# Attention beginnings in a written order, statistics, mixes and sums in other places, last batch on VectorE

## The chip, the cores and the metric

One core of a Trainium2 chip runs the whole program. Its engines are TensorE (PE in the profile; PEld is its weight load), VectorE (DVE), ScalarE (ACT), GpSimd (POOL) and SyncE (SP), which issues the DMAs. Each engine works through its own instructions in a fixed order and waits on semaphores for the others. The metric is the device time of one execution in microseconds (us): 1452.35 us, the median of three runs from 1451.99 to 1453.28. By the spread of these runs, a difference below some 0.2% can't be told from none.

## The reference

Everything is float32. x is 8 batches of 512 tokens with 512 channels (B, S, D); the context is 8 x 120 x 512. Four layers follow each other, each added to x through the tanh of a gate:

```python
x = x + jnp.tanh(g_xattn[0]) * _L0_xattn_ref(_layernorm(x), ctx, ctx, ...)       # 16 heads of 32, 120 keys
x = x + jnp.tanh(g_ffn[0])   * _L0_ffn_ref(_layernorm(x), Wc, bc, W1, b1, ...)   # routed: 32 tokens a group, 128 experts
x = x + jnp.tanh(g_xattn[1]) * _L1_xattn_ref(_layernorm(x), ctx, ctx, mask, ...) # with a mask and biases
x = x + jnp.tanh(g_ffn[1])   * _L1_ffn_ref(_layernorm(x), W_r, W_k, W_v, ...)    # mixes with the previous token:
    # xr = mu_r*x + (1-mu_r)*x_prev; out = sigmoid(xr @ W_r.T) * (square(relu(xk @ W_k.T)) @ W_v.T)
```

## The kernel before

x stays in SBUF as 32 tiles (NT) of 128 tokens by 512 channels; four tiles (TB) are a batch. Layernorm of a tile is `stats` (L372: `bn_stats` and `bn_aggr` on DVE, L49 and L50; after the fourth tile of a batch four small POOL instructions, the scales, L58 to L64) and `normalize` (L385: one ACT instruction, and in the second attention layer a POOL addition of the output bias to x, L394).

**Attention** (class CrossAttention, used twice). The constructor is its beginning. `load` issues the DMAs. `project_keys` transposes the context batch by batch (PE, L317, tile ctps), copies the result to ctxT (DVE L324 for even batches, ACT L322 for odd ones), and after each four batches makes half of the keys (PE L330, tile kps, 16 matrix products; ACT writes kT, L339 or L343). `project_values` makes the values of one batch (PE L349, tile vps; DVE L358 or L360). `prologue` interleaves values, the transposes of the first eight tiles of x (PE L405, tile xnps), the first queries and the scores of tile 0. `sum_query_weights` is four POOL instructions (L88). The key, value, transpose, query and output tiles share four PSUM banks (pool at_mm): a product waits until the bank four tiles back was read.

`run` is a loop of slots t, one for each tile of x: scores of tile t+1, queries ahead, output of tile t-1 (PE L582, DVE L591), transposes of the probabilities of tile t, its attention (PE L565, ACT aT L573). `tail` does the slots from 27 to 32, where no queries are left. Scores (L459 on): DVE takes two maxima (L498, L509), ACT exponentials (L501, L512), POOL normalizes (L491). `then` hands each slot to the next layer's `in_slot`, at stages 0 to 3 of the slot.

**Products of seven** (class SevenProducts). A 512x512x512 product is made from seven half-size ones, p1 to p7, with sums of quarters ahead (L88, L107) and additions after each (L169 to L202); two of the additions after p7 are on POOL (L191, L192). Queries, and all three products of the last layer, are made so.

**Channel mix** (class ChannelMix), the last layer. Its first batch is prepared in the last slots of the second attention (`in_slot`): key weight sums on POOL, mixes (`mix_chunk`: ACT L1161, DVE L1164), sums of the mix (L107 on DVE), p1 to p3 of the keys, sums of the other weights (`sum_weights`). It also takes the statistics of each tile two slots back. `run` then loops over the batches: keys, gates, values, where `stage` deals out the steps of a list over the seven products. `values` ends with the gate (DVE L1238), the addition to x (POOL L1241, for half of the last batch DVE) and the DMA of the result.

**Order of the work.** Inside `manual_schedule(engines=...)` the named engines get their instructions in the order of the calls. For engines that aren't named, a planner with its own costs orders them when the program is built. Before the change PE is in written order everywhere, SP in the second attention, the experts and the channel mix, and DVE, ACT and POOL only in the tails and in the channel mix's `run`; in both beginnings the planner places them.

## Time and profile before

| what | us |
|---|---|
| median of the runs | 1452.35 |
| the profiled execution, its own time | 1454.12 |
| its span | 1452.3 |
| PE busy | 1391.5 (96%) |
| DVE busy | 1021.2 (70%) |
| ACT busy | 768.9 (53%) |
| POOL busy | 653.0 (45%) |

The span is cut by stage like this: the first beginning from 0 to about 90 us, the slots of the first attention to about 475, the experts to 697, the second beginning to about 785, its slots to 1082, its tail to 1148, the channel mix to the end. In a timeline row the first number is the start, the second the length, then engine, line, operation, output and input tile, shapes and the number of instructions put together; the brackets give the engine's idle time just before and what ended it. In a row of a stretch each engine has its busy time and its instructions; the number after POOL is the granted clock of TensorE as a share of full speed, the last two are DMA.

### The profile page before, as it was taken

What the parts mean: (1) busy time and instruction counts of PE and PEld (TensorE: products, weight loads), DVE (VectorE), ACT (ScalarE), POOL (GpSimd) and SP (SyncE); (2) the same over time, 40 slices, a digit from 0 to 9 for tenths busy, and PEclk for the clock granted to TensorE, in tenths of its full rate; (3) what the DMA queues carried; (4) which work ended last, traced back from release to release, by engine and by line L of the source; (5) the groups of instructions that cost most, each with busy time, mean ns of one, the idle gap of its engine ahead of it and who ended that gap; (6) DMA issues with size and microseconds to landing.
All of it is one profiled execution on the core that took longest, in us unless ns stands there. A gap on an engine that the chain in (4) does not pass through costs nothing.

```text
span 1452.3 us, 32575 instructions
## 1 busy us (share of the span) xinstructions
PE 1391.5 (96%) x13728; PEld 1071.6 (74%) x13728; DVE 1021.2 (70%) x1449; ACT 768.9 (53%) x1874; POOL 653.0 (45%) x584
## 2 busy tenths in 40 slices
PE   6999999999999988999799999999998999999997
PEld 3477777777776777888457777777775688888886
DVE  2557767777776776777615788777779677777786
ACT  1256666666666445444225666566565554545543
POOL 2235545545544001555515676666546333333332
PEclk9999999999999999999999999999999999999999
DMA  9200000000001356433301000000000000000001
GB/s 301 100 9 23 23 23 23 24 23 23 23 23 46 125 155 206 118 103 85 115 0 59 2 1 2 1 2 2 2 30 2 1 29 29 30 30 30 30 17 43
DMA packets 44886, 69.46 MB, mean 48 GB/s; under 512 B 2891, under 2 KB 20811, under 8 KB 44739
## 3 DMA queue, kind: packets, MB, share of 16 engines
q1 hardware_dynamic: 44451, 67.37, 14.4%
q8 instruction: 108, 1.77, 0.5%
q14 instruction: 39, 0.32, 0.1%
q10 hardware_dynamic: 288, 0.00, 0.0%
HBM read 50.59 MB, written 16.78 MB: 46 GB/s over the span
## 4 chain that ended last, share of the span: by engine, by line
PE 29%; DVE 11%; ACT 5%; issue 3%; POOL 2%; POOLq 0%; DVEq 0%; ACTq 0%
PE qps L148 7%; PE ops L582 6%; PE cps L148 3%; PE tps L530 3%; PE kps L330 2%; PE vps L349 2%; PE aps L565 2%; PE s L473 2%; DVE xk L1164 2%; DVE xr L1164 1%; ACT kT L1214 1%; DVE cv L1238 1%; ACT pr L501 1%; PE xnps L405 1%; DVE xks L107 1%
## 5 line engine op out<-in xcount | busy, mean ns | idle before, releaser
L491 POOL TENSOR_TENSOR pr<-pr,rs 128x960 f32<-128x960 f32 x128 | 229.7, 1797 | 233.3 <-DVE rs L490 214.8
L582 PE MATMUL ops<-wo,aT 128*128 128x512 f32 x512 | 239.8, 595 | 3.0 <-ACT aT L573 3.0
L501 ACT ACTIVATE pr<-s,nmx 128x120 f32<-128x120 f32 x512 | 176.3, 370 | 118.2 <-DVE nmx L498 118.2
L582 PEld LDWEIGHTS ops<-wo,aT 128*128 128x128 f32 x512 | 92.0, 190 | 74.8 <-issue 67.0
L991 POOL TENSOR_TENSOR r<-r,b 128x1024 f32<-128x1024 f32 x31 | 73.6, 2378 | 145.5 <-ACT r L990 145.5
L148 PE MATMUL qps<-xnT,wq 128*128 128x256 f32 x512 | 119.6, 381 | 0.0
L530 PEld LDWEIGHTS tps<-ident,pr 128*120 128x120 f32 x864 | 96.8, 138 | 28.4 <-issue 24.8
L501 ACT ACTIVATION_READ_ACCUMULATOR pr<-s,nmx 128x1 f32 x512 | 111.1, 217 | 0.0
L509 DVE TENSOR_REDUCE mx<-s 128x8 f32<-128x960 f32 x64 | 74.0, 1156 | 51.6 <-PE s L473 51.6
L148 PEld LDWEIGHTS qps<-xnT,wq 128*128 128x128 f32 x512 | 95.7, 189 | 15.2 <-issue 1.0
L530 PE MATMUL tps<-ident,pr 128*120 128x128 f32 x864 | 104.8, 273 | 1.7 <-ACT pr L501 1.5
L49 DVE BATCH_NORM_STATS2 bnst<-x 128x6 f32<-128x512 f32 x128 | 84.5, 684 | 15.7 <-DMA x<-in_x_dram 14.3
L517 DVE TENSOR_REDUCE sm<-pr 128x8 f32<-128x960 f32 x64 | 73.6, 1149 | 23.5 <-ACT pr L512 23.5
L406 ACT COPY xnT<-xnps 128x512 f32<-128x512 f32 x64 | 38.0, 594 | 84.9 <-PE xnps L405 84.9
L565 PE MATMUL aps<-prT,v 120*32 120x128 f32 x2048 | 73.2, 278 | 4.9 <-ACT prT L555 3.0
L498 DVE TENSOR_REDUCE nmx<-s 128x8 f32<-128x960 f32 x64 | 73.4, 1147 | 5.7 <-PE s L473 5.7
L1241 POOL TENSOR_TENSOR x<-x,cv 128x512 f32<-128x512 f32 x30 | 44.0, 1466 | 72.0 <-DVE cv L1238 72.0
L511 DVE TENSOR_TENSOR pr<-s,mx 128x960 f32<-128x960 f32 x64 | 73.5, 1149 | 0.8
L540 ACT COPY prT<-tps 120x1024 f32<-120x1024 f32 x54 | 55.0, 1018 | 33.5 <-PE tps L530 33.5
L473 PE MATMUL s<-kT,qT 32*128 32x120 f32 x2048 | 71.6, 277 | 0.0
L473 PEld LDWEIGHTS s<-kT,qT 32*128 32x128 f32 x2048 | 66.3, 188 | 6.5 <-issue 6.3
L565 PEld LDWEIGHTS aps<-prT,v 120*32 120x32 f32 x2048 | 53.8, 110 | 19.1 <-issue 8.4
(184 smaller groups left out, 3111.9 us busy)
## 6 DMA issues: line engine op xcount, KB each, us to landing
w<-in_w_dram SPq DMA_DIRECT2D x32, 512.0 KB, 4.9
x<-in_x_dram SPq DMA_DIRECT2D x8, 1024.0 KB, 14.8
aside<-x SPq DMA_DIRECT2D x32, 256.0 KB, 2.0
x<-aside SPq DMA_DIRECT2D x8, 1024.0 KB, 10.2
out_dram<-x SPq DMA_DIRECT2D x14, 512.0 KB, 2.8
ctx<-in_ctx_dram SPq DMA_DIRECT2D x4, 960.0 KB, 11.7
wk<-in_wk_dram SPq DMA_DIRECT2D x3, 1024.0 KB, 11.3
wv<-in_wv_dram SPq DMA_DIRECT2D x3, 1024.0 KB, 5.9
```

The lines of the kernel that those rows point to most:

```text
L49: cm.nc.vector.bn_stats(st, cm.x[:, t, :])
L148: self.nc.tensor.matmul(ps[:, m, :], self.a[a][:, k, m * P : (m + 1) * P], self.b[b][:, k, :], start=(k == 0), stop=(k == 1),)
L473: nc.tensor.matmul(s[j // 2][:, j % 2, hc * LK : (hc + 1) * LK], self.qT[b][r : r + 32, hc, toks], self.kT[r : r + 32, hc, keys], start=no ...
L491: nc.gpsimd.tensor_tensor(pr[:, js, :, :], pr[:, js, :, :], rs[:, js, :, :].to_broadcast([P, 2, NC, LK]), ALU.mult,)
L501: nc.scalar.activation(pr[:, 2 + j, hc, :], sv[1][:, j, hc, :], AF.Exp, bias=nmx[:, j, hc, :], accum_out=sm[:, 2 + j, hc : hc + 1],)
L509: nc.vector.tensor_reduce(mx, sv[0], AX.X, ALU.max)
L511: nc.vector.tensor_tensor(pv, sv[0], mx.to_broadcast([P, 2, NC, LK]), ALU.subtract)
L517: nc.vector.tensor_reduce(sm[:, :2, :], pv, AX.X, ALU.add)
L530: nc.tensor.transpose(ps[:, jj, hc * P : (hc + 1) * P], pr[:, 2 * u + jj, hc, :], self.cm.ident,)
L565: nc.tensor.matmul(aps[32 * j : 32 * j + 32, hc, :], self.v[b // 2][:LK, b % 2, h * HD : (h + 1) * HD], prT[:, j, hc, :], start=True, stop ...
L582: nc.tensor.matmul(ops, self.aT[t][:, c, :], self.wo[:, c, :], start=(c == 0), stop=(c == NC - 1),)
L991: nc.gpsimd.tensor_tensor(r, r, b2, ALU.add)
```

## The change

No instruction is added or taken away in kind and count; they are put in other places and on other engines.

- Both beginnings are built with all five engines in written order. Statistics go by batch: batch 0 behind the last context copy in `project_keys`, batches 1 and 2 after the first normalizations, batches 3 to 7 each behind a value copy. `run` has no statistics any more. In the second beginning, scaling of the biases, of the output bias and the mask's row each get a place of their own, and the mask's DMA goes ahead of those of the output bias and of wq. The normalization of the scores of tile 0 goes behind the last two values, and the query sums of batch 1 go from POOL to DVE.
- In the last slots of the second attention, the statistics of tiles 24 to 31 go into the first four `values` of the channel mix, two tiles each. The four key mixes are spread over slots 27 (two), 28 and 29. The sums of the key mix go from DVE to POOL. The mixes and normalizations behind the keys' p5 in slot 31 go behind the attention of that slot. The sums of the value weights go from slot 32 to the start of slot 31.
- In `values` of the last batch, the two additions of p7 and all additions to x are on DVE.

```diff
@@ SevenProducts
-    def __init__(self, nc, psum, a, b, c, spare, finish=None, order="1265743", bias=None):
+    def __init__(self, nc, psum, a, b, c, spare, finish=None, order="1265743", bias=None, engine=None):
+        self.engine = engine or nc.gpsimd
...
-        nc.gpsimd.tensor_tensor(self.c[1, 1], u3, self.q5, ALU.add)
-        nc.gpsimd.tensor_tensor(u2, u2, self.q5, ALU.add)
+        self.engine.tensor_tensor(self.c[1, 1], u3, self.q5, ALU.add)
+        self.engine.tensor_tensor(u2, u2, self.q5, ALU.add)
@@ CrossAttention.__init__
                 self.load(ins, list(loads), mask, biases)
+                if self.biased:
+                    self.scale_biases()
                 self.project_keys()
-                for t in range(TB):
-                    self.stats(t)
+                if self.biased:
+                    nc.gpsimd.tensor_scalar(self.gbo, self.gbo, self.gate, None, ALU.mult)
                 for t in range(2):
                     self.normalize(t)
+                if self.masked:
+                    self.make_mask()
                 self.sum_query_weights()
+                for b in (1, 2):
+                    self.stats_of_batch(b)
@@ load (scale_biases and make_mask get its last instructions)
+        if self.masked:
+            nc.sync.dma_start(out=self.mrow, in_=mask.partition_broadcast(P))
+        if self.biased:
             self.gbo = self.pool.tile([P, D], FP, name="gbo")
             nc.sync.dma_start(out=self.gbo, in_=bo_in.partition_broadcast(P))
         weights(self.wq, wqT)
...
-        if self.masked:
-            nc.sync.dma_start(out=mrow, in_=mask.partition_broadcast(P))
         weights(self.wo, woT)
@@ project_keys
+            if b == B - 1:
+                self.stats_of_batch(0)
             if b % 4 == 3:
@@ project_values
+        if b + 3 < B:
+            self.stats_of_batch(b + 3)
@@ prologue
-        for t in range(TB, 2 * TB):
-            self.stats(t)
         for t in range(2 * TB):
             self.transpose_x(t)
-            self.stats(t + 2 * TB)
             self.normalize(t + 2)
...
-        self.scores(0)()
+        rest = self.scores(0)
         for b in range(B - 2, B):
             self.project_values(b)
-
+        rest()
+
+    def stats_of_batch(self, b):
+        for i in range(TB):
+            self.stats(TB * b + i)
@@ start_queries
-        engine = self.nc.gpsimd if b > 0 else self.nc.vector
+        engine = self.nc.gpsimd if b > 1 else self.nc.vector
@@ CrossAttention.run
-                if t + 16 < NT:
-                    self.stats(t + 16)
@@ ChannelMix: sum_weights becomes sum_gate_weights (wr, DVE) and sum_value_weights (wv, POOL); in_slot
-        if stage == 2 and 0 <= s - 2 < NT - 2:
+        if stage == 2 and 0 <= s - 2 < NT - 2 * TB:
             attention.stats(s - 2)
+        if stage == 2 and s == NT - 1:
+            for c in range(NC):
+                self.mix_chunk(0, 0, c)
+            for t in range(TB, 2 * TB):
+                self.normalize(t)
         if stage == 0:
             if s == NT - 1:
+                self.sum_value_weights()
                 self.k7.next()
...
+        for c in {NT - 5: (0, 1), NT - 4: (2,), NT - 3: (3,)}.get(s, ()):
+            self.mix_chunk(0, 1, c)
         if s in (NT - 5, NT - 4):
-            for c in range(2 * (s - NT + 5), 2 * (s - NT + 5) + 2):
-                self.mix_chunk(0, 1, c)
+            for _ in range(2):
                 self.weight_sums.pop(0)()
         if s == NT - 3:
-            self.key_sums = self.sum_steps(0, 1)
+            self.key_sums = self.sum_steps(0, 1, nc.gpsimd)
...
         if s == NT - 1:
             self.k7.next()
-            for c in range(NC):
-                self.mix_chunk(0, 0, c)
-            for t in range(TB, 2 * TB):
-                self.normalize(t)
         if s == NT:
             self.k7.next()
-            self.sum_weights()
-            for t in (NT - 2, NT - 1):
-                attention.stats(t)
+            self.sum_gate_weights()
@@ values
-            (nc.vector if last and i == 0 else nc.gpsimd).tensor_tensor(xs, xs, c, ALU.add)
+            (nc.vector if last else nc.gpsimd).tensor_tensor(xs, xs, c, ALU.add)
...
-        return self.product(a, self.wv7, places, finish, order=order)
+        engine = nc.vector if last else nc.gpsimd
+        return self.product(a, self.wv7, places, finish, order=order, engine=engine)
@@ ChannelMix.run
+            if b < TB:
+                t = NT - 2 * TB + 2 * b
+                work += calls(self.at.stats, *[(t + i,) for i in range(2)])
             self.stage(self.values(b), work)
@@ flamingo_kernel
+    every = compute | {engines.SP}
...
-            with tc.manual_schedule(engines={engines.PE}):
+            with tc.manual_schedule(engines=every):
                 attention = CrossAttention(
...
+            with tc.manual_schedule(engines={engines.PE}):
                 attention.run()
...
-        with tc.manual_schedule(engines={engines.PE, engines.SP}):
+        with tc.manual_schedule(engines=every):
             attention = CrossAttention(
...
+        with tc.manual_schedule(engines={engines.PE, engines.SP}):
             attention.run()
```

## The prediction

> **What bounds the kernel now.** I read the busy time by stage first: PE is busy 36.30 of 36.30 us in nearly every slice of the slots, and about 36.1 in the channel mix. In the slots no other engine's time can be turned into gain. What PE loses is some 61 us of idle time and a few stretches at half clock, so the second view is that of PE's waits:
>
> ```profile
> PE ctps L317 <- DMA ctx<-in_ctx_dram: 9.4, 1, 9.4
> PE kps L330 <- ACT ctxT L322: 9.4, 4, 7.4
> ...
> PE tps L551 <- DVE x L591: 3.3, 3, 2.2
> PE aps L565 <- ACT prT L555: 3.0, 3, 1.2
> PE ops L582 <- ACT aT L573: 3.0, 3, 1.8
> ...
> PE ctps L317 <- ACT kT L343: 2.2, 2, 1.6
> ...
> PE tps L530 <- ACT pr L501: 1.5, 3, 0.7
> ```
>
> The change touches all of these but the first (the first DMA) and the last. Third, the timeline of the two beginnings: ACT in the first, then ACT, DVE and PE in the second.
>
> ```profile
> 27.74 0.81 ACT L390 ACTIVATE xn<-x,nmr,rstd 128x512 f32<-128x512 f32 x1 [6.96 <-POOL nmr L64]
> 28.46 0.55 ACT L343 ACTIVATE kT<-kps 128x480 f32<-128x480 f32 x1
> 31.84 15.79 PE L330 MATMUL kps<-ctxT,wk 128*128 128x480 f32 x32 [0.65 <-ACT ctxT L322]
> ...
> 703.52 1.52 ACT L390 ACTIVATE xn<-x,nmr,rstd 128x512 f32<-128x512 f32 x2 [10.46 <-POOL nmr L64]
> 704.07 0.64 DVE L324 COPY ctxT<-ctps 128x480 f32<-128x480 f32 x1
> 706.78 14.52 PE L330 MATMUL kps<-ctxT,wk 128*128 128x480 f32 x32 [7.42 <-ACT ctxT L322]
> ```
>
> In both, ACT stood still for statistics while finished PSUM tiles waited for its copies; PE starved behind it. Fourth, TensorE's clock (the number after POOL's work): 0.52 behind the waits of 1.6 and 0.5 for kT, 0.56 behind the 7.42, 0.60 behind a stretch in which PE worked 0.68 of 4.00 us:
>
> ```profile
> 31.80:37.40 5.60, 5.56 (x8) 2.52 (x8) 4.13 (x13) 0.00 (x0) 3.54 (x7) 0.52 1.05 387
> 706.70:710.00 3.30, 3.22 (x5) 1.64 (x6) 3.30 (x11) 0.00 (x0) 1.64 (x5) 0.56 0.69 253
> 1097.70:1101.70 4.00, 0.68 (x5) 0.44 (x5) 3.72 (x6) 4.00 (x17) 1.04 (x1) 1.00 0.00 0
> 1101.70:1104.00 2.30, 2.22 (x32) 1.48 (x32) 1.58 (x3) 1.64 (x3) 2.30 (x2) 0.60 0.03 7
> ```
>
> **First beginning.** In written order ACT does each kT copy when its product ends (the third and fourth at 23.5 and 26.7), and no normalization stands before them. The second ctps then follow the first kps at 26.6. Their cost with copies is known from the second beginning, where nothing interferes: kps ended at 721.3, the next began at 723.60, so 2.3 to 2.5 us. The second kps starts at 29.1 instead of 31.84 (2.7), and at full clock, as after that same gap at 723.60, takes 13.15 instead of 15.79 (2.6). **Gain 5.35.** Ends: 2.7 (clock still halved) and 5.6. Behind it DVE owes batch 0 behind the copies (29 to 31.5; four `bn_stats` with `bn_aggr` are 2.8 by the rows at L49), batches 1 and 2 by 38, and each later batch behind a value copy: 2.8 + 0.69 = 3.5 against PE's 3.87 per value and transpose (58.20 to 62.07). DVE keeps up, and the last x had landed by 47.6 before. ACT normalizes tiles 0 and 1 at 43, PE wants them at 52. SP's order here is the one that the row order shows already.
>
> **Second beginning.** ctps end at 699.36, DVE's last addition to x at 698.7; two copies each on DVE and ACT take until 700.0. kps start there instead of at 706.78 (6.7), and at full clock (14.52 to 13.15, 1.4). **Gain 8.05.** Ends: 0, if the copies are still late, and 8.3. The scaled key bias that ACT now waits for is two POOL instructions of 0.2 right behind the experts' last addition (695.5; bqk lands at 696.7), wanted at 703. A wait is added on POOL: the additions of gbo to tiles 0 and 1 wait for ACT's normalizations, which stand behind the last kT copy (729.3). Queued behind them are the four query weight sums (5.2), which end at 738; PE wants them at 754.7. Scales for batches 1 to 7 (1.96 each, 701.52 to 703.48) follow, mixed with 1.27 additions: batch 1 at 740 (wanted by ACT at 746), batch 7 at 754, when POOL has caught up. On SP the mask (480 KB, 9.3 us to land) goes ahead of gbo and wq. Both come later by at most that, about 713 and 720, wanted by POOL at 720 and 733. If this cover were gone, PE would stop at its second pair of query products by the lateness; 16 us are free.
>
> **Scores of tile 0.** Batch 1's sums cost DVE two of 0.69 ahead of the maxima (and two later) in each beginning. Written order takes L498 first where the planner took L509 first (774.70, then 775.77), so ACT's exponentials start where they did. Recip and POOL's normalization move behind the last value copy, 2.5 us later (784.0 to 786.6); PE transposes them at 790.29. I cost this at nothing. In `run` the statistics were done ahead of time (DVE's rows have none between 58 and 110), so nothing is saved there.
>
> **Tail of the second attention.** Each step is one stall, followed through:
> 1. Slot 27 loses one statistics step (1094.88 to 1095.70). The wait 2.18 of the fourth tps becomes 1.36: 0.8.
> 2. Slot 28 has one mix, not two, and no statistics. L498 came 1.16 after its scores (1107.16); now it waits for PE. The exponentials and copies behind it set the end, with the gain at 2.0.
> 3. Slot 29 loses two key sums and a statistics step (1113.46 to 1117.4) and gets one mix (about 2.0, as 1091.07 shows two at 3.89 beside POOL). The 0.72 wait goes: 3.3 at the end of attention 30.
> 4. Output 30 waits no more (0.53): kT's relu and square come earlier than aT is wanted.
> 5. Output 31 waits no more (1.76): mixes and normalizations now stand behind aT on ACT. Late next is DVE, which does four mixes before p7's addition, 1137.4; p3 ends at 1142.2, where gates begin. Before that was 1148.20: 6.0.
> 6. The wait for wrs (0.53) goes: DVE's sums end 0.3 before PE wants them.
>
> **Gain 6.5.** POOL takes the key sums (1.6 each, by L88's rows here) and all value sums by 1132, before the mixes at 1134.7. Ends: 3.6 (steps 1, 4, 5, 6 alone) and 8.2, if the half-clock stretch 1101.7 to 1106 (4.3 us at 0.6, 1.7) goes too. I take it to stay: its gap shrinks from 2.18 + 1.16 to 1.36 + 1.16 within 3.2 us, and between 26.9 and 30.3 PE was 35% busy and went to half clock all the same. In a sentence of its own: the Trainium skill (TensorE: Matmul & The Clock Gate, "HAM oscillation") puts the limit at idle gaps above some 3.4 us; by that no gap here halves the clock, and the sum would have 8.2 here. The trace disagrees, as its 2.18 gap did halve it.
>
> **Channel mix.** Two statistics steps come into each of the first four `values`, behind p4 and p3. The next keys hang on DVE there:
>
> ```profile
> 1218.38 1.26 DVE L1238 SCALAR_TENSOR_TENSOR cv<-cv,gates,r 128x512 f32<-128x512 f32 x1
> 1219.56 2.42 DVE L1164 SCALAR_TENSOR_TENSOR xr<-yT,mu,xr 128x512 f32<-128x512 f32 x2
> ...
> 1231.33 0.67 DVE L202 TENSOR_TENSOR kT<-kT,cps 128x512 f32<-128x512 f32 x1
> 1232.06 1.99 PE L148 MATMUL cps<-wrs,xrs 128*128 128x256 f32 x8
> ```
>
> PE's product at 1232.06 waits for the bank that L202 reads (0.27 idle), and L202 is the end of a chain without slack back to POOL's additions at 1215.91. Two steps are 1.7. But the 1.26 and 2.42 are 0.75 and 1.41 stretched by POOL's additions beside them, and `bn_stats` was not stretched beside POOL's sums at 28.24 (1.29 for two). A step in front of each lets POOL finish: stretched work ends at 1222.5 instead of 1221.98. **Loss 0.55 x 4 = 2.2**; ends 0 and 6.8.
>
> **Last batch.** From L184 (1438.59) DVE does 14 instructions without waits: by the pitches here (0.60 independent, 0.72 and 0.79 behind the one before) the last addition starts at 1447.63 instead of 1448.41. **Gain 0.8**; ends 0 and 1.5.
>
> **Sum.** 5.35 + 8.05 + 6.5 - 2.2 + 0.8 = 18.5. The profiled execution was 1454.12, with 1.8 around its span of 1452.3; it would be 1435.6. The median of the runs, 1452.35, is 1.8 below the profiled time, so it becomes 1433.8.
>
> **Rivals.**
> - *Full clock, hidden statistics* (0.15). The tail's clock stays up, because the shorter gap is too short to halve it, and the channel mix hides its steps: 1433.8 - 1.7 - 2.2 = 1429.9. Against it: the 35% above and the 0.27 wait. The rule of the Trainium skill named above speaks for the first half.
> - *Statistics paid in full* (0.15). `bn_stats` is stretched beside two-input POOL work or nothing is displaced: 1.7 x 4 instead of 0.55 x 4, 1438.4.
> - *The second beginning stays late* (0.10). The order binds only what is inside; if the planner puts other work of DVE or ACT ahead of the copies, all 8.05 go: 1441.9. Against: nothing but the last addition at 697.96 is left to do.
> - *All gains are given back* (0.03): copies late in both beginnings (13.4), the tail at its low end (2.9) and statistics paid in full (4.6): 1433.8 + 20.9 = 1454.7, no change.
> - *Slower: the planner* (0.07). It lays out DVE, ACT and POOL in both `run` loops anew from another start. The first slots show a wait of 0.7 for pr; one such wait in each of 54 slots is 37.8: 1471.6. It decides from (18.5 + 2.9) / 54 = 0.40 us a slot. Against: both layers, planned from different starts, keep PE at 36.30 of 36.30, with DVE at 26 to 30.
>
> **How the numbers follow.** The forecast has 0.50, its own range 1431 to 1437. The range 1428 to 1443 takes in the first three rivals and leaves the last two. Differences within 0.2% (2.9 us) are about what can't be told from none. Faster: 0.50 + 0.15 + 0.15 + 0.10 = 0.90; same 0.03; slower 0.07.
>
> **What would show it.** First beginning: no PE wait behind kT copies, both kps rows near 13.15. Second: kps 0.65 after ctps, clock 1.0. Tail: gates 6 to 8 us nearer to the first tail slot's scores, no wait of ops on aT. Mix: PE waits of about 0.8 instead of 0.27 in the gates of batches 1 to 4, and 0.27 after. The end: POOL idle in the last values. The forecast is wrong if PE's waits in the slots grow, or if POOL's queue holds the query sums past 16 us.

## The result and the profile after

The kernel after takes 1442.56 us (median of four runs, 1440.98 to 1444.58) against 1452.82 for the kernel before, run beside it: a ratio of 0.9929, 95% interval 0.9911 to 0.9946. That is 10.3 us faster, where 18.5 were forecast. The profiled execution took 1441.8, its span 1440.0; against the span of 1452.3 before that is 12.3, because the execution profiled before lay 1.3 above its median and this one 0.8 below.

All line numbers are those of the kernel after, unless a row is said to be of the kernel before. From L317 on they are some 10 to 17 higher than before (L317 is now L327, L330 L342, L551 L567), up to L202 at most one. PE's waits after the change, total, number and longest in us:

```profile
PE cps L149 <- DVE kT L203: 4.0, 4, 1.0
PE aps L581 <- ACT prT L571: 2.7, 3, 1.2
PE kps L342 <- ACT ctxT L332: 2.6, 4, 0.6
...
PE tps L567 <- DVE x L607: 1.4, 1, 1.4
...
PE qps L149 <- DVE xnT L107: 1.1, 1, 1.1
PE qps L149 <- POOL nmr L64: 1.1, 1, 1.1
PE tps L546 <- DVE pr L527: 1.0, 2, 0.6
```

The wait of kps for the context copies went from 9.4 to four times 0.65, that of ctps for kT is gone, and ops no longer waits for aT in the tail. Outside the experts four entries are larger or new: cps for kT (the channel mix), qps twice, and tps for pr at L527. Each is a piece of the gain that was given back. PE's timeline in the beginnings:

```profile
13.44 15.47 PE L342 MATMUL kps<-ctxT,wk 128*128 128x480 f32 x32 [0.65 <-ACT ctxT L332]
...
31.20 13.15 PE L342 MATMUL kps<-ctxT,wk 128*128 128x480 f32 x32 [0.65 <-ACT ctxT L332]
...
697.48 13.15 PE L342 MATMUL kps<-ctxT,wk 128*128 128x480 f32 x32 [0.65 <-ACT ctxT L332]
...
712.92 13.15 PE L342 MATMUL kps<-ctxT,wk 128*128 128x480 f32 x32 [0.65 <-ACT ctxT L332]
```

Three of four kps rows run at full pace behind a wait of 0.65. The first is 2.32 longer. It ran at 13.15 before, but with the same code in front it does so in five of nine traces of this study and not in the other four (e8 below), so it is taken as chance and not as an effect of the change; of the kernel before there is one trace only.

PE's milestones cut the span into stages. Four of the eight stages (values to first transposes, the second beginning, its slots, and first to last gates) take the same time, to 0.1 us, in all traces of this study that have the same code there, so they can be compared where whole runs scatter by 3 to 4 us. The first stage and the tail take a few fixed values, by TensorE's pace at the start and by its clock. In us (the boundaries are the first value product, the first transposes of probabilities, the second ctps, the first transposes of the second attention, the end of its query products, the first and the last batch's gates):

| stage | before | after | gain | forecast |
|---|---|---|---|---|
| start to first values | 47.46 | 44.18 | 3.28 | 5.35 |
| values to first transposes | 52.99 | 55.05 | -2.06 | 0 |
| slots and experts | 597.05 | 595.75 | 1.30 | 0 |
| second beginning | 92.79 | 86.07 | 6.72 | 8.05 |
| its slots | 285.68 | 285.77 | -0.09 | 0 |
| tail, to the first gates | 72.23 | 65.01 | 7.22 | 6.0 |
| first gates to last gates | 271.19 | 275.62 | -4.43 | 0.5 - 2.2 |
| last gates to the end | 32.91 | 32.55 | 0.36 | 0.8 |
| sum | 1452.3 | 1440.0 | 12.3 | 18.5 |

The slots of the first attention with the experts are the one stage that scatters with no cause in the change that the traces show: 593.5 to 597.2 in twelve traces with the change (the kernel after and eleven of its variants), 597.05 before. Two things that differ can be seen there: PE's waits called "issue" (1.21 in one trace, 0.88 in another, at the start of the experts' gathers), and a clock of 0.79 to 0.91 in some 8 us of the same place in some of the traces.

### The profile page after: what moved, and what is told of

The parts are those of the page before. It is cut to its first block, busy times and chain, and to the rows that moved or that the text cites. A ratio compares the mean times of both kernels' runs of the same rounds, so it can differ in the third digit from the quotient of the medians.

```text
span 1440.0 us, 32567 instructions
## 1 busy us (share of the span) xinstructions
PE 1386.5 (96%) x13728; PEld 1067.2 (74%) x13728; DVE 1022.6 (71%) x1457; ACT 770.6 (54%) x1874; POOL 643.4 (45%) x576
## 4 chain that ended last, share of the span: by engine, by line
PE 71%; DVE 15%; ACT 6%; POOL 4%; issue 3%; DMA 1%; POOLq 0%; DVEq 0%; ACTq 0%
PE ops L598 14%; PE qps L149 13%; PE tps L546 6%; PE cps L149 5%; PE aps L581 4%; PE s L489 4%; PE kps L342 4%; PE rps L992 3%; PE vps L361 3%; PE rlps L731 2%; PE l1ps L907 2%; PE ops L1013 2%; DVE rT L972 2%; PE xnps L421 2%; PE gps L880 2%
## 5 line engine op out<-in xcount | busy, mean ns | idle before, releaser
L527 DVE TENSOR_TENSOR pr<-s,mx 128x960 f32<-128x960 f32 x64 | 73.5, 1149 | 0.9
L1258 POOL TENSOR_TENSOR x<-x,cv 128x512 f32<-128x512 f32 x28 | 39.7, 1416 | 71.9 <-DVE cv L1255 71.9
```

What stands on the lines that cost most here:

```text
L527: nc.vector.tensor_tensor(pv, sv[0], mx.to_broadcast([P, 2, NC, LK]), ALU.subtract)
```

## The experiments

The theory from the profile of the kernel after had five parts: (1) written order in the second beginning brought its gain, (2) the written order of query sums gave 1.1 back in each beginning, (3) the channel mix pays 0.78 a batch for the way the key-mix sums are dealt and 0.53 for the statistics, (4) the tail's gain comes from statistics and arrangement together and its clock is chance, (5) the first kps at half pace are chance too. Ratios are to the kernel before, timed beside each; the kernel after stands at 0.9929. Their intervals reach 0.0012 to 0.0023 to either side.

**e4: the second beginning left to the planner.**

```diff
-        with tc.manual_schedule(engines=every):
+        with tc.manual_schedule(engines={engines.PE, engines.SP}):
             attention = CrossAttention(        # the second one
```

> The beginning of the second attention keeps its new written sequence, but only TensorE's and the DMA queue's orders are held; ACT, DVE and GpSimd are placed by the planner there. Theory: the written order of ACT and DVE (copies of the context ahead of statistics and normalizations) is what brought the 7.3 us by which the second beginning is shorter; without it the wait of kps for the copies of some 7 us is back, kps run near 14.5 us instead of 13.15, and the time is 7 to 8 us above the kernel after: 1450, a ratio near 0.998. Rival: the moved statistics alone emptied the place ahead of the copies, so that the planner would have come out as well: no wait of kps over 1 us, and the time within 1 us of 1442.6.

Measured: 1446.14, ratio 0.9966 (0.9954 to 0.9979), 5.4 us worse than after by the ratios. The beginning takes 92.78, to 0.01 us what it took before. The timeline of e4, ACT and PE:

```profile
699.86 1.52 ACT L406 ACTIVATE xn<-x,nmr,rstd 128x512 f32<-128x512 f32 x2 [10.46 <-POOL nmr L64]
701.29 0.99 ACT L332 COPY ctxT<-ctps 128x480 f32<-128x480 f32 x2
...
703.12 14.52 PE L342 MATMUL kps<-ctxT,wk 128*128 128x480 f32 x32 [7.42 <-ACT ctxT L332]
```

ACT waits 10.46 us for statistics with the copies behind it, exactly as before the change. So the second beginning's gain needs the written order; the moved statistics without it bring none. A written order without the moved statistics was not run. The copies' part is 7.42 - 0.65 + 14.52 - 13.15 = 8.14, which is what the forecast had (8.05). The stage gained only 6.70, so the written order gave 1.44 back behind it. (By run times 7 to 8 us were expected and 5.4 measured; the stage's 6.70 is the firmer number.)

**e1: the third query sum ahead of p2's addition.**

```diff
+        if f == 0 and b == 0:
+            for step in self.later_sums:
+                self.q7.next()
+                step()
+            return
         self.q7.next(2 if f < TB - 1 else 1)
```

> The four products of the second query weight sum (T2) come ahead of the second half of tile 0's projection (p2) in both attentions, where after the change they stand behind it; nothing else changes. Theory: the waits of 1.1 us that the written order brought (of qps for DVE's addition in the first attention, of the same product for the sums' reader in the second) were paid because T2's place behind p2 made PE stand for p2's addition. Both go: the scores of tile 0 begin 1.1 us earlier in each attention, 2.2 us in all, 1440.4 against the 1442.6 of the kernel after, and a ratio to the kernel before near 0.9914. Rival: the wait only moves to the next product that reads the same buffer (T4, or the scores themselves), and the time stays within 0.5 us of 1442.6.

(T2 is a sum of quarters of x, made by DVE at L107; a product of the query weight sums, wqs, reads it.) Where the 1.1 comes from, in the timeline of the kernel after, DVE and PE:

```profile
70.26 0.69 DVE L170 TENSOR_TENSOR qT<-qT,qps 128x512 f32<-128x512 f32 x1 [1.49 <-PE qps L149]
70.87 1.41 DVE L107 TENSOR_TENSOR xnT<-xnT 128x512 f32<-128x512 f32 x2
...
71.70 1.96 PE L149 MATMUL qps<-xnT,wqs 128*128 128x256 f32 x8 [1.11 <-DVE xnT L107]
```

and before the change, at the same place:

```profile
71.35 1.49 DVE L107 TENSOR_TENSOR xnT<-xnT 128x512 f32<-128x512 f32 x2
73.54 0.69 DVE L169 TENSOR_TENSOR qT<-qT,qps 128x512 f32<-128x512 f32 x1 [0.69 <-PE qps L148]
...
73.70 1.89 PE L148 MATMUL qps<-xnT,wqs 128*128 128x256 f32 x8
```

Before, the second of the two sums at 71.35 is the one that PE's product needs, and it is done ahead of p2's addition at L169. After the change, DVE stands idle for 1.49 until PE has finished p2, adds it, and only then makes that sum. (The trace puts the like wait in the second attention down to POOL, L64; it falls from 1.11 to 0.20 by this edit, which moves DVE's sums alone.)

Measured with the sum first: no wait at that product (69.94) in the first attention; values to first transposes 53.69 instead of 55.05, second beginning 85.16 instead of 86.07; together 2.27 of the expected 2.2. The time was 1439.29, ratio 0.9905 (0.9891 to 0.9919).

Of the 2.06 in the first beginning 0.70 remain: the wait of 0.56 of the first tps for pr stays (0.55, and 0.45 in the second beginning). The traces show what delays it. This tps takes over a PSUM buffer of the scores of tile 1 (both are tiles of the pool at_s), so it waits until DVE has read those scores, at L527. POOL and DVE ahead of that, in the kernel after:

```profile
93.55 1.79 POOL L507 TENSOR_TENSOR pr<-pr,rs 128x960 f32<-128x960 f32 x1 [0.80 <-DVE rs L506]
...
94.19 1.70 DVE L107 TENSOR_TENSOR xnT<-xnT 128x512 f32<-128x512 f32 x1
95.81 1.15 DVE L525 TENSOR_REDUCE mx<-s 128x8 f32<-128x960 f32 x1
```

The scores of tile 1 are there at 95.03, but DVE starts on them at 95.81. It is held up by a query sum of batch 1, which the change gave to DVE, and which takes 1.70 instead of 0.68 beside POOL's normalization of tile 0, which the change put behind the last value copy. Where the planner orders these engines (e5b below), POOL has finished at 91.74, the same sum takes 0.68, and the first tps waits for nothing. That this is the cause is read from the traces; no run moves these two steps alone.

**e5 and e5b: the first beginning left to the planner.** The same edit as e4 on the first attention, with TensorE alone in written order.

> The beginning of the first attention keeps its new sequence, but only TensorE's order is held; ACT, DVE, GpSimd and the DMA queue are placed by the planner there, as before the change. Theory: as in the second beginning, it was the order written for ACT (the copies of keys ahead of normalizations) that took the waits of 1.6 and 0.5 for kT away; the statistics were moved in the sequence as well, so the planner finds less ahead of the copies than before the change, and I expect a part of the waits back: first values at 44 to 47 us instead of 41.7 (a start at full clock) or 44.2 (at half), the end 2 to 5 us above the kernel after, 1445 to 1447, a ratio near 0.996. Rival: the planner comes out the same from the new sequence: no wait for kT, the time within 1 us of 1442.6, a ratio near 0.993.

Measured: 1443.15, ratio 0.9929 (0.9915 to 0.9942), no difference to after. Since that can be no effect or two that cancel, a further run gives a trace of it.

> The kernel of e5 once more, for its trace: its runs were at 1439 to 1443 as those of the kernel after are. Theory (that was the rival): the moved statistics alone emptied ACT's queue ahead of the key copies in the first beginning, and the written order of ACT, DVE and GpSimd adds nothing there: no wait of ctps for kT, first values at 41.7 (or 44 after a start at half pace).

Measured: 1440.25 in one run. First values at 44.04, and from there to the first transposes 52.98, as before the change, where the written order needs 55.05. ACT in that trace:

```profile
27.29 0.81 ACT L406 ACTIVATE xn<-x,nmr,rstd 128x512 f32<-128x512 f32 x1 [4.61 <-POOL nmr L64]
28.01 0.55 ACT L355 ACTIVATE kT<-kps 128x480 f32<-128x480 f32 x1
```

The planner again puts a normalization ahead of a copy of keys (27.29, before the change 27.74). PE shows no wait for it, but this run started at half pace (kps 15.38), and its third product ended later than in a run at full pace; so the trace does not show the copy to be harmless. Written orders that also started at half pace are the ones to compare it with (the kernel after and e10: kps 15.47 and 14.95). Without the first kps and what stands ahead of it, the way to the first values takes 15.53 in e5b against 15.27 and 15.28, so the written order gains 0.25 there; behind the first values it loses 2.06. After a slow start it thus costs 1.8 in all. Without it the stage up to the first transposes ends at 97.0, with it at 96.6 to 96.9 or, after a slow start, at 98.5 to 99.2. What the planner's order would do at a full-pace start, where the copy at 28.01 could hold PE up as before the change, has no trace, and the whole runs show no difference. So neither theory is shown: the normalization is ahead of the copy again, but neither a wait nor a loss for it is in the trace.

**e2 and e3: who pays in the channel mix.** e2 deals the values' steps by hand, two sums in the first turn and one in each that follows, with the statistics where the change has them; e3 also moves the statistics into turns in which DVE waits.

```diff
-                work += calls(self.at.stats, *[(t + i,) for i in range(2)])
+                work = [work[:2]] + [[step] for step in work[2:]]
+                for i in range(2):
+                    work[5 + i].append(lambda t=t + i: self.at.stats(t))
```

and in e3, in place of the last two lines and ahead of the gates' stage:

```diff
+                work[4].append(lambda t=NT - 2 * TB + 2 * b + 1: self.at.stats(t))
...
+            if b < TB:
+                turns[6].insert(0, lambda t=NT - 2 * TB + 2 * b: self.at.stats(t))
             self.stage(self.gates(b), turns)
```

> In the channel mix the ten steps of the values' seven turns (four key-mix sums, four normalizations, two statistics steps) are dealt so that the first turn has two sums, the next two have one each, and the statistics stay where the change has them, in the last two turns with the normalizations. The kernel after deals ten steps evenly, so that its first two turns and one more have two. Theory: of the 1.31 us that each of the first four batches lost, 0.78 came from that dealing (a fourth sum beside GpSimd's addition, right ahead of the additions that the key products hang on) and 0.53 from the statistics. The distance of the gates from batch to batch goes from 40.04 to 39.26 us, 3.1 us in all, 1439.5 and a ratio near 0.9908. Rival: the statistics alone, by their place behind p4 and p3, cost all of 1.31: the distance stays at 40.0 and the time at 1442.6.

> As the dealing of sums in e2, and the two statistics steps of a batch are taken out of the last two turns of the values: one goes into the turn where DVE waits 1.45 us for GpSimd, one into the last turn of the gates, where DVE waits 1.31 us for ACT. Theory: both steps (0.83 each) then lie in time that DVE has, and the distance of the gates from batch to batch is 38.73 us again, 5.2 us less in all than after the change: 1437.4, a ratio near 0.9893. The difference to e2 is then the statistics' own price, some 0.53 a batch. Rival: the whole chain from GpSimd's additions on is full (no wait there is free time, since its own end is awaited): the distance is 39.3 or more, as in e2.

The distance from one batch's gates to the next was 38.73 before (the first 38.80); after the change it is 40.04 four times, behind the first. Measured: 39.24 in e2, so the dealing costs 0.80 a batch and the statistics in these places 0.51. The time of e2 was 1440.65, ratio 0.9916 (0.9903 to 0.9928); the whole runs show 1.9 of its 3.1 us, but they scatter by more than that (1435.48 to 1440.89). In e3 the distances alternate, 38.74, 39.54, 38.74, 39.56; the time was 1436.40, ratio 0.9892 (0.9879 to 0.9905). Both the theory (38.73) and its rival (39.3 or more) came true, in turn. What differs between the two kinds of batch is POOL, which after every fourth tile makes the scales in the middle of the values (POOL's timeline of e3):

```profile
1195.33 1.26 POOL L193 TENSOR_TENSOR cv<-cv,q 128x512 f32<-128x512 f32 x1
1196.67 0.56 POOL L58 TENSOR_SCALAR ve<-mv 128x4 f32<-128x4 f32 x1
1197.31 1.04 POOL L59 TENSOR_TENSOR rstd<-ve,mhalf 128x4 f32<-128x4 f32 x1
...
1198.92 4.62 POOL L1258 TENSOR_TENSOR x<-x,cv 128x512 f32<-128x512 f32 x3
```

The additions to x begin 3.59 us behind the one at L193, against 1.90 in the next batch (1234.87 and 1236.77); three of them run on end, and DVE's two mixes beside them take 3.43 instead of 2.42. The next keys pay for it, one batch later.

**e10: the scales where POOL has nothing.** As e3, but the step that completes four tiles stands in the next batch's gates.

```diff
+            if 0 < b <= TB:
+                turns[6].insert(0, lambda t=NT - 2 * TB + 2 * b - 1: self.at.stats(t))
             self.stage(self.gates(b), turns)
...
+                work[4].append(lambda t=NT - 2 * TB + 2 * b: self.at.stats(t))
```

> As e3 (sums of the key mix dealt in the old turns), but the first of a batch's two statistics steps stands in the values' turn where DVE waits for GpSimd, and the second, which completes four tiles and is followed by GpSimd's four instructions for their scales, stands in the last turn of the next batch's gates, where GpSimd has nothing. In e3 those scales came amid the values every second batch, held GpSimd's additions up by 2.1 us, and the gates' distance was 38.73 and 39.55 in turn. Theory: those 0.81 come from GpSimd's scales between its additions; with the scales moved every distance is 38.73 us: 1.6 us less than e3 and 5.2 less than the kernel after, 1437.3 by the median after, a ratio near 0.9885. Rival: the 0.8 belong to the statistics step itself in the gates (DVE), which now falls into four batches as well: distances of 39.5 remain.

Measured: 38.75, 38.75, 38.74, 38.75. The first to the last gates take 270.47, 0.72 less than before the change. The time was 1436.24, ratio 0.9893 (0.9878 to 0.9908), though its profiled execution had a half-pace start and a halved clock in the tail. Against e3 (1436.40) whole runs show no difference; the distances do. So the statistics cost nothing in the mix once they lie where DVE and POOL both have time. DVE in the values of the kernel after:

```profile
1193.83 0.68 DVE L107 TENSOR_TENSOR xks<-xk 128x512 f32<-128x512 f32 x1
1194.43 1.76 DVE L107 TENSOR_TENSOR xks<-xks,xk 128x512 f32<-128x512 f32 x1
1196.12 0.67 DVE L175 TENSOR_TENSOR cv<-cv,cps 128x512 f32<-128x512 f32 x1
1196.89 0.69 DVE L185 TENSOR_TENSOR cv<-cv,cps 128x512 f32<-128x512 f32 x1
1199.03 1.74 DVE L1255 SCALAR_TENSOR_TENSOR cv<-cv,gates,r 128x512 f32<-128x512 f32 x1 [1.45 <-POOL cv L192]
```

And the same place in e10:

```profile
1195.56 0.68 DVE L107 TENSOR_TENSOR xks<-xk 128x512 f32<-128x512 f32 x1
1196.17 0.68 DVE L175 TENSOR_TENSOR cv<-cv,cps 128x512 f32<-128x512 f32 x1
1196.76 1.17 DVE L107 TENSOR_TENSOR xks<-xks,xk 128x512 f32<-128x512 f32 x1
1197.86 0.68 DVE L185 TENSOR_TENSOR cv<-cv,cps 128x512 f32<-128x512 f32 x1
1198.46 0.68 DVE L49 BATCH_NORM_STATS2 bnst<-x 128x6 f32<-128x512 f32 x1
1199.17 0.18 DVE L50 BATCH_NORM_AGGREGATE mv<-bnst 128x2 f32<-128x6 f32 x1
1199.98 1.74 DVE L1255 SCALAR_TENSOR_TENSOR cv<-cv,gates,r 128x512 f32<-128x512 f32 x1 [0.62 <-POOL cv L192]
```

After the change the fourth sum stands directly behind the third, beside POOL's addition to x (1193.99 to 1195.64), and takes 1.76; L175, and L185 behind it, come late, and POOL's additions and the next keys hang on L185. One place further, as in e10 and before the change, it takes 1.17 and the addition goes first. The statistics fill 0.83 of DVE's wait of 1.45.

**e7: the tail's arrangement as before.** The mixes, sums and normalizations of the last slots go back to their old places and engines; the statistics stay away. The edit is the reverse of the diff's part on `in_slot`, without its first line.

> The last slots of the second attention get back the arrangement of before (both mixes of a slot, key sums on DVE, weight sums, mixes and normalizations ahead of output 31); their statistics stay away, in the channel mix. Theory: of the tail's gain (70.7 us from the end of the slots' queries to the last output before, 63.5 after), the statistics alone are steps 1 and a part of 2, some 1.6 us, and the arrangement is the rest: the stretch is 68 to 70 us, and the time 4.5 to 6.5 us above the kernel after, 1447 to 1449, a ratio near 0.997. Rival: the statistics were what made the slots late, and the arrangement moves work that was hidden: the stretch stays under 65 us, the time within 1.5 us of 1442.6.

Measured: 1444.86, ratio 0.9955 (0.9938 to 0.9971), 3.8 us worse than after by the ratios; 69.54 from the end of the queries to the last output (70.66 before, 63.44 in the kernel after). PE's waits in the tail of the kernel after:

```profile
1080.86 1.56 PE L581 MATMUL aps<-prT,v 120*32 120x128 f32 x32 [0.71 <-ACT prT L571]
1089.93 0.65 PE L567 MATMUL tps<-ident,pr 128*120 128x128 f32 x4 [1.37 <-DVE x L607]
1091.75 1.56 PE L581 MATMUL aps<-prT,v 120*32 120x128 f32 x32 [1.17 <-ACT prT L571]
1100.73 1.56 PE L581 MATMUL aps<-prT,v 120*32 120x128 f32 x32 [0.84 <-ACT prT L571]
```

And of e7, from the second on:

```profile
1086.55 0.65 PE L567 MATMUL tps<-ident,pr 128*120 128x128 f32 x4 [1.39 <-DVE x L607]
1088.35 2.41 PE L581 MATMUL aps<-prT,v 120*32 120x128 f32 x32 [1.15 <-ACT prT L571]
1099.72 1.56 PE L581 MATMUL aps<-prT,v 120*32 120x128 f32 x32 [0.34 <-ACT prT L571]
1107.92 0.65 PE L567 MATMUL tps<-ident,pr 128*120 128x128 f32 x4 [0.49 <-DVE x L607]
1115.69 3.70 PE L598 MATMUL ops<-wo,aT 128*128 128x512 f32 x8 [0.52 <-ACT aT L589]
...
```

Its last is 1.76 at output 31. The clock was halved behind the second of these waits in e7 (aps takes 2.41 instead of 1.56), as in the kernel before and in e4, for 3.41 us before and for 6.83 in the other two. The waits sum to 8.59 before, to 6.35 in e7 and, with the new arrangement, to 3.60 in e4 (0.71, 1.37, 1.17 and 0.35). The statistics' move is worth 2.24 of it and the arrangement 2.75: 0.49 at the last tps, 0.52 and 1.76 at the two outputs. With the clock up, as in the kernel after, the sum is 4.09, since aps comes earlier and waits 0.84. The stage itself takes 72.23 before, 71.11 in e7 and 67.76 in e4. From before to e7 it gains only 1.12, as half clock lasts 3.41 us longer in e7 and costs 1.7 more; from e7 to e4, with half clock alike, it gains 3.35.

**e8: TensorE kept busy before the context lands.**

```diff
+        if not self.biased:
+            ps = self.p_mm.tile([P, NC, P], FP, name="warm", tag="mm")
+            for c in range(26):
+                nc.tensor.matmul(ps[:, c % NC, :], ident, ident, start=True, stop=True)
```

> 26 identity products that nobody reads are added at the start of the first attention, before the context has landed; nothing else changes. In two of five traces with the new beginning the first kps took 15.3 to 15.5 us, their first products at half pace, in three 13.15. Theory: TensorE's clock at that point depends on how long it has worked when kps begin; with the added products it is up in every run, kps take 13.15, and the first values start at 41.7 in each: 2.2 us less in the runs that were slow, 1 us in the median (1441.5), with less spread. Rival one: the added products delay the first transposes and the gain is lost: the first ctps at 10 or later. Rival two: it has another cause, and kps run at 13.15 or 15.4 by chance as before.

The stretch in which the first kps begin, in the kernel after (from:to, its length, PE busy with its matmul records, PEld, DVE, ACT, POOL, then the granted clock, DMA share, GB/s):

```profile
13.20:17.60 4.40, 4.17 (x6) 1.85 (x6) 0.00 (x0) 0.18 (x1) 0.00 (x0) 1.00 1.05 252
```

and in e2:

```profile
13.20:17.60 4.40, 4.34 (x11) 2.20 (x12) 0.00 (x0) 0.57 (x2) 0.00 (x0) 1.00 1.06 250
```

Six products against eleven in the same time, with a granted clock of 1.00 in both rows: here the record of the clock does not show the half pace, and the number of products does. Without the added products kps started so in four of nine traces (14.95 to 15.47), with the same code in front. With them the first kps took 13.15 in all three traces that have them, and started 0.7 to 1.2 earlier, as the transposes ran at full pace too (1.81 to 1.86 instead of 3.26 to 3.44 in all nine). Three full-pace kps in a row would come by chance in some 17% of cases ((5/9) cubed); it is the transposes, slow in nine of nine and fast in three of three, that show the added products to work. In e8's trace first values came at 40.88, 3.3 before those of the kernel after. The time was 1437.69, ratio 0.9901 (0.9888 to 0.9914), the four runs within 1.5 us. That is 4.9 us below the kernel after, where 1 was expected; the first stage accounts for 3.3 against a half-pace start and 0.7 to 0.9 against a full-pace one, and the rest is not shown to come from this edit.

**e6: the last batch's additions on GpSimd again.** One condition back in `values`, and `engine = nc.gpsimd`.

> The last batch's additions are back on GpSimd (its first two quarters' additions to x, as before the change, and its two bank sums). Theory: from PE's last product to the end of the span it takes 8.57 us again, as before the change, against 8.21 after it: 0.36 us. Rival: the order of the products, that the change left as it was, sets the end, and it stays at 8.2.

Measured: from the last gates to the end 32.92, as before (32.91); 8.59 behind PE's last product, as expected. After the change this stage takes 32.55 in two traces and 32.2 in the nine others, so the part is worth 0.36 to 0.7.

**e11 and e12: the edits together.** e11 is e1, e10 and e8 in one kernel; e12 adds 8 products ahead of the third transposes of slot 27.

```diff
+            if self.masked and t == NT - TB - 1 and j == 0:
+                for c in range(8):
+                    nc.tensor.matmul(ps[:, c % NC, :], ident[:, :LK], ident, start=True, stop=True)
```

> Three edits of the experiments before in one kernel: T2 ahead of p2 (e1), the dealing of sums and statistics of e10, and the unread products ahead of the first attention (e8). Theory: each took away a wait of its own stage, and the stages follow one another, so the savings add: 2.3 (by the milestones of e1), 5.2 (by the gates' distance in e10) and 2.2 in a run that would have started at half pace: 1432 to 1434 against the 1442.6 of the kernel after, a ratio near 0.987, and no run above 1437 but where the tail's clock halves. Rival: part of the savings is the same time (the DVE work that T2 no longer waits for comes back as a wait in the first slots): 1435 or more, a ratio above 0.988.

> e11 and one thing more: 8 identity products that nobody reads, some 0.9 us, ahead of the third transposes of slot 27 in the second attention, where the fourth transposes then wait 1.37 us for DVE and the attention behind them 1.17 us for ACT. In eight traces these two waits were the same to 0.02 us, and the clock was halved behind them in four (some 2.7 us) and not in the other four. Theory: the clock is halved when PE's idle share in some window of its own is too high, and the window's place is chance; with the filler in the place of 0.9 us of the first wait the idle share falls from 2.5 of 4.2 us to 1.6, the clock stays at 1.00, the last output comes 63.5 us after the end of the slots' queries, and no run of the five is 2.7 us above the others: 1432 to 1433. Rival: the filler delays the copies that the attention waits for, and the wait of 1.17 grows by as much; or the planner lays out the slots anew and time is lost there.

Measured: e11 1430.08, ratio 0.9847 (0.9824 to 0.9870); e12 1430.06, ratio 0.9845 (0.9825 to 0.9865). The savings add: e11 is 12 us below the kernel after and 23 below the kernel before run beside it, more than the theory had. In its trace the first values come 3.3 earlier than in the kernel after, and the stages of e1 and e10 are 1.35, 0.87 and 5.19 shorter; the remaining 2.3 to the 13.0 between the two spans are mostly the scatter of the experts' stage. Between e11 and e12 there is nothing to tell. The clock in the tail of the kernel after:

```profile
1088.50:1092.50 4.00, 1.38 (x18) 0.81 (x21) 3.44 (x6) 4.00 (x13) 1.77 (x2) 1.00 0.00 0
1092.50:1096.50 4.00, 4.00 (x71) 2.68 (x61) 3.66 (x3) 1.42 (x5) 3.92 (x4) 1.00 0.02 4
```

of e4, the same stretch:

```profile
1094.04:1098.04 4.00, 1.39 (x19) 0.82 (x22) 3.43 (x6) 4.00 (x13) 1.78 (x2) 1.00 0.00 0
1098.04:1102.04 4.00, 4.00 (x67) 3.03 (x56) 2.65 (x2) 0.89 (x2) 3.92 (x4) 0.55 0.01 4
1102.04:1106.04 4.00, 4.00 (x7) 1.67 (x6) 2.70 (x3) 3.42 (x17) 0.79 (x1) 0.59 0.00 0
```

and of e12:

```profile
1083.70:1087.70 4.00, 2.65 (x27) 1.90 (x29) 3.46 (x6) 4.00 (x13) 1.75 (x1) 1.00 0.00 0
1087.70:1091.70 4.00, 4.00 (x71) 2.70 (x64) 3.63 (x3) 1.42 (x5) 3.92 (x4) 1.00 0.00 0
```

After and e4 are busy for the same 1.38 and 1.39 of four us, with the same waits; one keeps its clock, the other runs at half for 6.83 us and loses 2.75 (tail of 67.76 against 65.01). Of the ten traces with the tail's new arrangement and no filler, five halved there, at 1.5 to 2.75 us each. e12's filler lifts PE's share from 1.4 to 2.65 without making the tail longer (65.01). Its one trace shows no such loss and its five runs lie within 2.4 us (1429.14 to 1431.52), but e11's trace has none either, so that the filler prevents it is not shown.

## Why the prediction was partly right

The 1442.56 lies outside the forecast's own range (1431 to 1437) and 0.4 inside the upper end of the wide one (1443). It is closest to the 1441.9 of the rival "the second beginning stays late", which is not what happened: the copies there gained 8.14. Chance has a share as well: the profiled execution lost 2.3 by its half-pace start and won 1.7 by a clock that stayed up in the tail.

- **First beginning.** What it forecast is in the trace: no ctps waits for kT, the second kps start 0.65 behind their copies at 13.15. That the written order is needed for it is not shown (e5b). At a full-pace start first values come at 41.6 to 41.8 (five traces), a gain of 5.7 to 5.9 where 5.35 was the term. The profiled run had a half-pace start (4 of 9) and 3.28. The forecast saw half clock only in the second kps, where a wait had halved it, and not that the start itself is a matter of chance.
- **Scores of tile 0**, "I cost this at nothing": this is the step that failed. It looked at ACT and at the maxima, and not at the order on DVE between p2's addition and the sums that PE's next product reads. It cost 2.06 in the first beginning and 1.44 in the second; e1 gets 1.36 and 0.91 back. The rest, some 0.7 and 0.5, is a second oversight: the prediction followed the delayed normalization only to tile 0's own transposes, and not to the sum that DVE makes beside it and to tile 1's maxima behind that.
- **Second beginning.** The copies' 8.05 are right (8.14 by e4); 6.72 is what is left of it after the step above. That it takes the written order was argued; e4 shows it. The rival that it stays late has its condition exactly there: ACT and DVE left to the planner. POOL's longer queue cost nothing, as worked out.
- **Tail.** Step 1 came out to the hundredth (2.18 to 1.37), and so did steps 4 and 5 (0.53 and 1.76). Steps 2 and 3 were mis-sized: the three waits 0.38, 1.16 and 0.72 shrank to 0.84, which is 1.4 (1.9 in e4, whose clock was halved), where the prediction had 2.5 for them (3.3 less 0.8). Its steps also add up to 5.6 (3.3, 0.53 and 1.76), so that its 6.0 holds 0.4 that no step names. By e7 the statistics did most of it (1.43), the places of mixes and sums 0.48. In the kernel after the waits make 4.5 of the 7.22. Another 1.7 came from a clock that was not halved this time (before, 3.41 us at 0.50); the last 1.0 was not taken apart. The forecast kept the halving with a reason ("35% busy"), its rival took it away with another; by ten traces the odds are even. The Trainium skill (TensorE: Matmul & The Clock Gate, "HAM oscillation") names idle gaps above some 3.4 us as the limit; e4's longest wait there is 1.37, and it halved, so that the trace does not bear it out. The same page of the Trainium skill (Part 1, on the clock gate) says that the activity window runs freely and isn't reset by the kernel; equal waits with unequal clocks agree with that.
- **The wait for wrs** (0.5 forecast) is gone: the first gates' distance went from 38.80 to 38.01, 0.79. It is 38.03 in e7 too, with the value weight sums in their old place; so it isn't the arrangement that did it; the two statistics steps that left this slot remain, and no run tests them alone.
- **Channel mix.** "Loss 0.55 x 4" is right for the statistics in these places (0.51 by e2), and `bn_stats` was indeed not stretched beside POOL (0.68 and 0.69). What was overlooked is that two steps more in the list shift the dealing of the other eight, which cost 0.80 a batch. So the loss was 5.2, in the reach of the rival "paid in full" (6.8), but not by its mechanism.
- **Last batch.** 0.36 in the profiled run, 0.7 in most others, of 0.8.
- **The planner as a danger.** The slots of the second attention take 285.77 instead of 285.68; nothing came of it.

The difference of 8.8 us between 1442.6 and 1433.8 is mostly made of these: 3.5 in the scores of tile 0, 3.0 in the mix, 1.0 to 1.5 in the tail (steps 2 and 3, and the 0.4); the remainder is within what start and clock change by chance from run to run.

## What to carry to other kernels

When an order is written out by hand, follow it on every engine it binds: a written order that frees one engine's copies can set another engine's sum behind an addition that waits, as here on DVE for 1.1 us, twice. When steps are added to a list that is dealt over turns, look first at where the old steps land; and place a step by its whole tail, the small instructions on another engine included. Compare stages between milestones of the bottleneck engine before comparing run times: here half of them repeat to 0.1 us where runs scatter by 4. When two variants are compared by one trace each, check first that they are alike in what changes by chance, such as a half-pace start.

## What the hardware showed that was not expected

- The pace of TensorE after its first transposes differs from run to run with the same code: eight products in 5.1 to 5.7 us against 3.3, with a granted clock of 1.00 in the record both times. With 7.4 us of unread products before it (at 1.36 to 8.79, e8; 8.6 and 8.8 us in e12 and e11) the transposes and the products behind them ran at full pace in three of three traces.
- Behind the same two waits (1.37 and 1.17 us within 3.2) the clock was halved in five traces out of ten. Every stretch at half clock that ended within a span lasted 3.41 or 6.83 us by the record of the clock: 17 of 17, in the traces of the kernel before and of eight of the variants.
- Two-input work of DVE beside POOL's two-input additions is not slowed by a factor: it ends 0.55 us behind the addition. In the trace of the kernel before this holds for all 66 sums, mixes and gate products (L88, L107, L1164, L1238) that began with over 0.4 us of such an addition still to run: they end 0.55 to 0.56 behind it, so that what takes 0.68 or 0.75 alone took from 1.00 to 2.27 there, the longer the earlier it began. `bn_stats`, with one input, kept 0.68 to 0.70 beside such additions.
